# Keys and queries as one Strassen product, norms after the first keys, short node scans and mixed queries two chunks ahead in a graph-transformer layer

## Chip, cores, metric

One core of a Trainium2 chip. The metric is the device time of one execution in microseconds. Engines are named as the profile names them: PE (TensorE, matmul), PEld (its weight loads), DVE (VectorE), ACT (ScalarE), POOL (GpSimd), SP (SyncE, which here only issues transfers).

## What is computed

10,000 nodes with 512 features, 160,000 edges sorted by the node that they point to. All numbers are float32.

```python
xn = layernorm(x)
# node part: rows gathered at the edges' sources, weighted, summed per target
node = relu(segment_sum((xn @ W)[edge_src] * edge_weight[:, None], edge_dst) + bias)
# linear attention, 8 heads of 64
q, k, v = split(xn @ w_qkv.T, 3)
q = softmax(q, over the 64 features of a head) * 64 ** -0.5
k = softmax(k, over all nodes)
mix = gamma_layernorm(((k.T @ v) per head applied to q) @ w_out.T, gamma)
x = x + node + mix
# feed-forward with 6 experts of 341 units, weights of the experts from the mean row
x = x + ffn(layernorm(x))
```

The edges are sorted by `dst`, the target; `src` is random. The sum commutes with the product by `W`, so the kernel sums gathered rows of `xn` first and multiplies the sums (by `wg`) later.

## The kernel before

The nodes are worked on in 20 chunks of 512 rows (the last has 272); a chunk lies in a tile [128 partitions, 4 rows, 512]. P = 128, SUB = 4, KB = 4 blocks of 128 features, KH = 2. There are three stages.

**1. Normalised rows.** All chunks are read, normalised and stored to `xn_d` in HBM. The first EARLY = 3 stay in SBUF, in a pool of 3 buffers; the others go through 4 buffers.

```python
def normal_rows(n):
    for c in range(len(normal), min(len(normal) + n, NCH)):
        xt = (xp if c < EARLY else a_io).tile([P, SUB, D], F32, name="xn")
        nc.sync.dma_start(xt[:r], tokens(x, c))
        row_stats(xt, r, mv, on_pool=True)
        ...                                   # 2 of 4 rows on ScalarE, 2 on GpSimd
        nc.scalar.dma_start(tokens(xn_d, c), xt[:r])
```

**2. Keys, with the edges between.** Per chunk: keys and queries (16 matmuls of 128x512 each), exponentials, `G += ek.T @ xn` (16 more), and 32 transposes. `usable` is 1 where the weights' norms are small enough for exponentials without a maximum; it comes from two squares and 8 matmuls at the start.

```python
norms(0, wk); norms(1, wq); as_they_are()        # gives `usable`
for c, (_, r) in enumerate(chunks):
    if c == EARLY:
        normal_rows(NCH); place_edges(); ...
        done[1] = -6 * PACE                      # edges begin
    for s in range(SUB):
        times(pk, xnT, s, r, wk)                 # 4 matmuls 128x512
        work(KB * PRODUCT)                       # PRODUCT = 0.83
        nc.scalar.activation(ek[:r, s, :], pk[:r], AF.Exp, scale=usable[:r])
        nc.vector.tensor_tensor(kacc[:r], kacc[:r], ek[:r, s, :], ALU.add)
    for s in range(SUB):
        times(pq, xnT, s, r, wq)
        work(KB * PRODUCT)
        ...                                      # exp, softmax of each head -> qt
    xnT = turned_rows(c + 1, xn_next)            # 16 transposes
    for cb in range(KB):
        for s in range(SUB):
            nc.tensor.matmul(pc, ek[:r, s, cb * P : (cb + 1) * P], xn[:r, s, :], ...)
        ...                                      # G += pc, work(...), qt transposed and stored
    find_rows(c, added)
```

The order of instructions on PE is that of the program; the other engines' order comes from a scheduler. An edge tile is 128 edges. `work(us)` tells how much of PE's own work has been put out, and edge tiles are put out behind it, one per PACE = 0.93 of that sum:

```python
def edges_in(i):                                 # one gather per edge tile, 128 rows of 2 KB
    m[k] = pools["m"].tile([P, D], F32, name="msg")      # 24 buffers
    nc.gpsimd.indirect_dma_start(out=m[k], in_=xn_d, in_offset=...src_sb[:, t0 + k]...)
    nc.vector.tensor_scalar(sel[:, k, 1:], iota_w, place..., w_sb..., op0=is_equal, op1=mult)
def edges_summed(i, batch, m, sel):              # 4 windows of 32 nodes side by side on PE
    nc.tensor.matmul(pm[h * 32 : (h + 1) * 32, :], sel[:, k, :], m[k], ...)
    nc.scalar.copy(part, pm); nc.scalar.dma_start(part_d[...], part)
def work(us):
    done[1] += us
    edges_to(groups_of(int(done[1] / PACE)))
```

A node that lies on the edge between windows is put together by `carry`: two loads from `part_d`, a product, a store. `find_rows` finds for every node its row in `part_d`, by a scan of all 802 windows:

```python
for s in range(SUB):
    nc.vector.scalar_tensor_tensor(past, bases[:, :NW], node[:, c, s : s + 1], jump,
                                   op0=ALU.is_le, op1=ALU.mult, accum_out=at[:, s : s + 1])
```

**3. Nodes and queries, with the rest of the edges between.** `attention(c)` multiplies the stored queries with the mixing matrix; `gathered(c)` fetches the chunk's node rows, once `far_enough(c)` has put out the edges that they need (all of them from chunk 18 on, where the edge buffers are given up and the experts' weights are loaded).

```python
def attention(c, beside):
    qT = queries_in(c); xt = rows_again(c)
    for s in range(SUB):
        if s == SUB - 1:
            beside()
        times(po, qT, s, r, mix); put_out(KB * PRODUCT)
        ...                                      # layer norm, gamma, + x  -> ot

ot_next = attention(0, lambda: None)
for c, (_, r) in enumerate(chunks):
    ot, at = ot_next, held["at"]
    def nodes_rows():
        transposed(aT, at, r, psum, "ps", by_act=range(KB))
        if c + 1 < NCH:
            held["at"] = gathered(c + 1)         # 4 gathers of node rows
    if c + 1 < NCH:
        ot_next = attention(c + 1, nodes_rows)
    else:
        nodes_rows()
    for s in range(SUB):
        times(po, aT, s, r, wg); put_out(KB * PRODUCT)
        ...                                      # bias, relu, added to ot
    nc.sync.dma_start(x1_d[c], ot[:r])
```

**4. Feed-forward**, 20 chunks again, with Strassen's products already; the change leaves it as it is.

Of the kernel before, what the change touches and what calls it, by code (L numbers as in the profile page):

```python
# [17 lines left out]
P = 128  # L18
SQ = 32
SUB = 4  # L20
EPS = 1e-5
HEAD = 64
# [5 lines left out]
EARLY = 3  # L28
ROWS_SOON = 5
PRODUCT = 0.83  # L30
PACE = 0.93

# [14 lines left out]
def gps_layer_kernel(  # L47
# [55 lines left out]
    nc.gpsimd.memset(ones, 1.0)  # L103
    zero = const.tile([P, D], F32, name="zero")
    nc.vector.memset(zero, 0.0)
    iota_w = const.tile([P, WIN - 1], F32, name="iota_w")
# [42 lines left out]
    by_window = part_d.rearrange("(w q) d -> w q d", q=WIN)  # L149
    nc.scalar.dma_start(part_d[ZERO_ROW : ZERO_ROW + P, :], zero)  # L150

# [30 lines left out]

    def softmax_rows(q, r, s, e=None):

        q3 = q[:r, s, :].rearrange("p (h e) -> p h e", e=HEAD)
        e3 = q3 if e is None else e[:r].rearrange("p (h e) -> p h e", e=HEAD)
        qs = small.tile([P, D // HEAD], F32, name="qs")
        nc.vector.tensor_reduce(qs[:r], e3, axis=AX.X, op=ALU.add)
        nc.vector.reciprocal(qs[:r], qs[:r])
        nc.vector.tensor_tensor(q3, e3, qs[:r, :, None].to_broadcast([r, D // HEAD, HEAD]), ALU.mult)  # L190

# [35 lines left out]
    def sums_for(o, b11, b12, b21, b22):  # L227

        return [nc.vector.tensor_tensor(o[0], b12, b11, ALU.subtract),
                nc.vector.tensor_tensor(o[2], b22, b12, ALU.subtract),  # L230
                nc.vector.tensor_tensor(o[1], b22, o[0], ALU.subtract),
                nc.vector.tensor_tensor(o[3], b21, o[1], ALU.subtract)]

    io_f = {}
# [100 lines left out]
    with ExitStack() as ph:  # L335
# [10 lines left out]
        keys_ctx = ph.enter_context(ExitStack())  # L346
        xp = keys_ctx.enter_context(tc.tile_pool(name="b_xn", bufs=EARLY, side="right"))
        b_io = keys_ctx.enter_context(tc.tile_pool(name="b_io", bufs=1, side="right", reuse_waits="tile"))
# [8 lines left out]
        def normal_rows(n):  # L357

            for c in range(len(normal), min(len(normal) + n, NCH)):
                r = chunks[c][1]  # L360
                xt = (xp if c < EARLY else a_io).tile([P, SUB, D], F32, name="xn")
                nc.sync.dma_start(xt[:r], tokens(x, c))
                mv = small.tile([P, SUB, 2], F32, name="mv")
                row_stats(xt, r, mv, on_pool=True)
                minus = small.tile([P, SUB], F32, name="minus")
                nc.vector.tensor_scalar(minus[:r], mv[:r, :, 0], -1.0, None, op0=ALU.mult)
                for i in range(SUB):
                    if i % 2:
                        nc.gpsimd.tensor_scalar(xt[:r, i, :], xt[:r, i, :], mv[:r, i, 0:1], mv[:r, i, 1:2],
                                                op0=ALU.subtract, op1=ALU.mult)  # L370
                    else:
                        nc.scalar.activation(xt[:r, i, :], xt[:r, i, :], AF.Identity, bias=minus[:r, i : i + 1])
                        nc.scalar.activation(xt[:r, i, :], xt[:r, i, :], AF.Copy, scale=mv[:r, i, 1:2])
                nc.scalar.dma_start(tokens(xn_d, c), xt[:r])
                normal.append(xt)

        normal_rows(2)
        wk = kvp.tile([P, KB, D], F32, name="wk")
        nc.sync.dma_start(wk, w_qkv_t[:, D : 2 * D].rearrange("(k p) d -> p k d", p=P))
        nc.sync.dma_start(wq, w_qkv_t[:, :D].rearrange("(k p) d -> p k d", p=P))  # L380
        wv = kvp.tile([P, KB, D], F32, name="wv")
        wo = kvp.tile([P, KB, D], F32, name="wo")
        src_sb = ep.tile([P, NET], I32, name="src_sb")
# [4 lines left out]
        jump = ep.tile([P, NW], F32, name="jump")  # L388
        count = ep.tile([P, 2 + len(AT_HAND)], F32, name="count")
        n_big = ep.tile([1, 2], F32, name="n_big")  # L390
# [3 lines left out]
        def place_edges():  # L394
# [11 lines left out]
            nc.vector.tensor_copy(bases[:, PAIRED:NW], row_sb[:, 2 * PAIRED :])  # L406
            gap = ew.tile([P, NW], F32, name="gap", tag="past", bufs=1)
            nc.vector.tensor_tensor(gap, bases[:, 1:], bases[:, :NW], ALU.subtract)
# [29 lines left out]
            for i, (n, w) in enumerate(AT_HAND):  # L438
                nc.vector.tensor_scalar(count[:, 2 + i : 3 + i], bases[:, w : w + 1],
                                        float(chunks[n][0] if n < NCH else N), None, op0=ALU.is_ge)  # L440

        ALL_GOOD = P * (NET + NW - 1 + len(AT_HAND))

        def find_rows(c, other):

            at = ew.tile([P, SUB], F32, name="at")
            for s in range(SUB):
                past = ew.tile([P, NW], F32, name="past", bufs=1)
                scan = nc.vector.scalar_tensor_tensor(
                    past, bases[:, :NW], node[:, c, s : s + 1], jump,  # L450
                    op0=ALU.is_le, op1=ALU.mult, accum_out=at[:, s : s + 1])
                if other:
                    behind(scan, other)
            nc.vector.tensor_tensor(at, at, node[:, c], ALU.add)
            nc.vector.tensor_scalar(row_of[:, c], at, float(ZERO_ROW), None, op0=ALU.min)
# [60 lines left out]
        def norms(i, w):  # L516

            sq = b_io.tile([P, KB, D], F32, name="sq", tag="ek")
            nc.scalar.activation(sq, w, AF.Square)
            pn = psum.tile([1, D], F32, name="pn", tag="ps")  # L520
            for kb in range(KB):
# [3 lines left out]
        def as_they_are():  # L525
# [3 lines left out]
            nc.vector.tensor_tensor(n_big[:, 0:1], n_big[:, 0:1], n_big[:, 1:2], ALU.mult)  # L529
            pn = psum.tile([P, 1], F32, name="pn", tag="ps")  # L530
            nc.tensor.matmul(pn, until[0:1, :], n_big[:, 0:1], start=True, stop=True)
# [87 lines left out]
        def all_edges(fp):  # L619

            earlier = fp.tile([P, P], F32, name="earlier")
# [103 lines left out]
        def rows_of(c):  # L727
            if c < EARLY:
                return normal[c]
# [8 lines left out]

        norms(0, wk)
        norms(1, wq)  # L740
        as_they_are()
        xn = rows_of(0)
        xnT = turned_rows(0, xn)
        for c, (_, r) in enumerate(chunks):
            if c == EARLY:
# [4 lines left out]
                for soon in range(ROWS_SOON):  # L750
# [4 lines left out]
                                                                 reuse_waits="tile"))  # L755
                nc.sync.dma_start(wv, w_qkv_t[:, 2 * D :].rearrange("(k p) d -> p k d", p=P))
                nc.sync.dma_start(wo, w_out_t.rearrange("(k p) d -> p k d", p=P))
            if c + 1 < NCH:
                xn_next = rows_of(c + 1)
            ek = b_io.tile([P, SUB, D], F32, name="ek")  # L760
            for s in range(SUB):
                pk = psum.tile([P, D], F32, name="pk", tag="ps")
                times(pk, xnT, s, r, wk)
                work(KB * PRODUCT)
                nc.scalar.activation(ek[:r, s, :], pk[:r], AF.Exp, scale=usable[:r])
                nc.vector.tensor_tensor(kacc[:r], kacc[:r], ek[:r, s, :], ALU.add)
            qt = b_io.tile([P, SUB, D], F32, name="qt")
            for s in range(SUB):
                pq = psum.tile([P, D], F32, name="pq", tag="ps")
                times(pq, xnT, s, r, wq)  # L770
                work(KB * PRODUCT)
                nc.scalar.activation(pq[:r], pq[:r], AF.Exp, scale=usable[:r])
                softmax_rows(qt, r, s, pq)
            if c + 1 < NCH:
# [15 lines left out]
            if c >= ROWS_SOON:  # L790
                find_rows(c, added)
            if c + 1 < NCH:
                xn = xn_next
        ps = psum.tile([P, KB], F32, name="pks", tag="ps")
        for cb in range(KB):
# [81 lines left out]
        def rows_again(c):  # L877
            xt = io.tile([P, SUB, D], F32, name="xt")
            nc.sync.dma_start(xt[: chunks[c][1]], tokens(x, c))
# [8 lines left out]
        def attention(c, beside):  # L888
# [4 lines left out]
            xt = rows_again(c)  # L893
            ot = io.tile([P, SUB, D], F32, name="ot", bufs=3)
            for s in range(SUB):
# [16 lines left out]

        ot_next = attention(0, lambda: None)
        for c, (_, r) in enumerate(chunks):
            ot, at = ot_next, held["at"]
            aT = io.tile([P, KB, SUB * P], F32, name="aT", bufs=1)
# [5 lines left out]

            if c + 1 < NCH:
                ot_next = attention(c + 1, nodes_rows)
            else:
# [170 lines left out]
    hp = ctx.enter_context(tc.tile_pool(name="f_h", bufs=1, reuse_waits="tile"))  # L1096

    def product(o, lhs, rhs, start=True, stop=True):  # L1100
        n = len(lhs)
        for j in range(n):
            nc.tensor.matmul(o, lhs[j], rhs[j], start=start and j == 0, stop=stop and j == n - 1,  # L1103
                             skip_group_check=True)

# [215 lines left out]
```

## Time and profile before

| what | value |
|---|---|
| time, median of 3 runs | 3378.7 us (3378.27 to 3379.26) |
| span of the profile, mean granted TensorE clock | 3379.6 us, 0.988 |
| busy: PE, DVE, ACT, POOL | 97%, 55%, 24%, 42% |
| first product of chunk 0 and of chunk 3 (keys) | 43.0 us, 193.2 us |
| first and last gather of an edge tile | 169.9 us, 1903.3 us |
| end of the last chunk's keys, first query product | 1137 us, 1180.2 us |
| last node product of the last chunk ends | 2009.6 us |
| gathers of edge tiles, of node rows | 1250, 80 |

A busy share is an average over the four stages. In the page's slices (84 us each) the keys run to the fourteenth, with edges between them from the third on, nodes and queries to the twenty-fourth, feed-forward from there on. A line of a group reads: source line, engine, operation, output<-inputs, shapes, count, then busy us and mean ns of one, then the idle time of the engine before it and who ended it. In the timeline a line is start, length, engine, source line, operation, and in brackets the idle time before and its releaser. A PE matmul of float32 appears as two records. A gather's line on POOL tells how long POOL was at it, not when its data landed.

### The profile page before, as it was taken

How to read it: one execution, taken by the hardware profiler on the slowest of the kernel's cores; microseconds unless marked ns; L12 is line 12 of the kernel's file. 1: busy time of each engine (PE TensorE's matmuls, PEld its weight loads, DVE VectorE, ACT ScalarE, POOL GpSimd, SP SyncE). 2: the span in 40 equal slices, each digit the busy share in tenths (PEclk: the TensorE clock that was granted, in tenths of full speed). 3: DMA queues.
4: the chain of work that ended last, by engine and by line, in shares of the span. 5: the costliest groups of instructions: out<-in, count | busy, mean ns of one | idle time of the engine just before them, and what ended most of it. 6: DMA issues, size and time to landing. Idle time of an engine off the chain costs nothing.

```text
span 3379.6 us, 37367 instructions
## 1 busy us (share of the span) xinstructions
PE 3270.7 (97%) x12969; PEld 1923.8 (57%) x12969; DVE 1842.5 (55%) x4771; ACT 797.3 (24%) x1626; POOL 1433.4 (42%) x1472
## 2 busy tenths in 40 slices
PE   6999999999999899999999999999999999999998
PEld 3444444444443333333333347888888888888886
DVE  7844545455545456666766576544554455445543
ACT  4412121212121121122222123222222222222211
POOL 6667777777777777777777420000000000000000
PEclk9999999999999999999999999999999999999999
DMA  9778888888878888999989751121212121212111
GB/s 363 262 231 254 275 258 279 257 272 263 268 241 262 290 291 304 309 329 325 329 313 329 235 163 50 50 63 50 88 50 63 54 84 50 63 60 78 50 39 40
DMA packets 218332, 644.96 MB, mean 191 GB/s; under 512 B 35486, under 2 KB 75422, under 8 KB 193786
## 3 DMA queue, kind: packets, MB, share of 16 engines
q0 software_dynamic: 108208, 354.02, 33.5%
q1 hardware_dynamic: 67656, 168.51, 15.2%
q10 hardware_dynamic: 42266, 119.91, 9.1%
q8 instruction: 106, 1.74, 0.2%
q14 instruction: 96, 0.79, 0.1%
HBM read 485.32 MB, written 157.00 MB: 190 GB/s over the span
## 4 chain that ended last, share of the span: by engine, by line
PE 54%; DMA 9%; issue 1%; DVE 1%; POOL 1%; ACT 0%; POOLq 0%; DVEq 0%; ACTq 0%; SPq 0%
PE px L1103 15%; PE pz L1103 10%; PE py L1103 10%; PE po L205 7%; DMA msg<-xn_d,src_sb 6%; PE pg L205 6%; PE pm L503 3%; PE ph L1103 2%; PE pt L197 1%; DMA z_d<-xt 1%; POOL msg L485 1%; DMA xt<-x_d 1%; DMA at<-part_d,row_of 1%; DMA x_d<-ot 0%; PE pcarry L568 0%
## 5 line engine op out<-in xcount | busy, mean ns | idle before, releaser
L485 POOL DMA_INDIRECT msg<-xn_d,src_sb x1250 | 1226.5, 981 | 424.8 <-issue 236.6
L503 PE MATMUL pm<-msg,sel 128*32 128x512 f32 x2504 | 356.2, 603 | 28.7 <-DMA msg<-xn_d,src_sb 28.6
L492 DVE TENSOR_SCALAR sel<-iota_w,place,w_sb 128x31 f32<-128x31 f32 x1250 | 305.9, 317 | 103.9 <-PE pm L503 103.7
L205 PE MATMUL po<-G,qT 128*128 128x512 f32 (+1 forms) x640 | 292.7, 604 | 8.0 <-DMA qT<-qT_d 8.0
L205 PE MATMUL pg<-wq,aT 128*128 128x512 f32 (+1 forms) x640 | 293.5, 607 | 5.9 <-ACT aT L199 5.9
L779 PE MATMUL pc<-xn,ek 128*128 128x512 f32 (+1 forms) x640 | 288.7, 601 | 3.7 <-DVE qt L190 3.7
L205 PE MATMUL pk<-wk,xnT 128*128 128x512 f32 (+1 forms) x640 | 285.7, 599 | 0.0
L205 PE MATMUL pq<-wq,xnT 128*128 128x512 f32 (+1 forms) x640 | 284.5, 597 | 0.0
L506 ACT COPY part<-pm 128x512 f32<-128x512 f32 x201 | 118.1, 587 | 629.7 <-PE pm L503 604.7
L503 PEld LDWEIGHTS pm<-msg,sel 128*32 128x32 f32 x2504 | 68.3, 109 | 282.2 <-issue 196.9
L205 PEld LDWEIGHTS pg<-wq,aT 128*128 128x128 f32 (+1 forms) x640 | 116.9, 189 | 182.9 <-issue 162.9
L205 PEld LDWEIGHTS po<-G,qT 128*128 128x128 f32 (+1 forms) x640 | 116.0, 189 | 171.0 <-issue 147.5
L205 PEld LDWEIGHTS pk<-wk,xnT 128*128 128x128 f32 (+1 forms) x640 | 118.1, 188 | 164.4 <-issue 153.1
L205 PEld LDWEIGHTS pq<-wq,xnT 128*128 128x128 f32 (+1 forms) x640 | 117.5, 187 | 165.3 <-issue 159.2
L1103 PE MATMUL px<-xnT,w_sb 128*128 128x256 f32 (+1 forms) x800 | 203.8, 377 | 6.4 <-DVE u L1138 6.3
L779 PEld LDWEIGHTS pc<-xn,ek 128*128 128x128 f32 (+1 forms) x640 | 118.7, 192 | 145.8 <-issue 141.7
L1103 PE MATMUL px<-w_sb,hh 128*128 128x256 f32 (+1 forms) x800 | 185.7, 379 | 0.0
L161 DVE BATCH_NORM_STATS2 st<-ot 128x6 f32<-128x512 f32 (+1 forms) x160 | 110.2, 689 | 138.4 <-ACT ot L903 137.5
L1103 PE MATMUL py<-xs,w_sum 128*128 128x256 f32 (+1 forms) x800 | 185.0, 374 | 0.0
L1103 PE MATMUL py<-w_sum,hh 128*128 128x256 f32 (+1 forms) x800 | 179.2, 379 | 0.0
L1103 PEld LDWEIGHTS px<-xnT,w_sb 128*128 128x128 f32 x800 | 150.3, 191 | 28.5 <-DVE u L1138 8.8
L1103 PEld LDWEIGHTS py<-w_sum,hh 128*128 128x128 f32 (+1 forms) x800 | 150.0, 188 | 22.7
(270 smaller groups left out, 4438.5 us busy)
## 6 DMA issues: line engine op xcount, KB each, us to landing
part_d<-part ACTq DMA_DIRECT2D x201, 256.0 KB
msg<-xn_d,src_sb POOLq DMA_INDIRECT x1250
xn<-in_x SPq DMA_DIRECT2D x19, 1024.0 KB
xn_d<-xn ACTq DMA_DIRECT2D x19, 1024.0 KB
qT_d<-qT ACTq DMA_DIRECT2D x19, 1024.0 KB
qT<-qT_d SPq DMA_DIRECT2D x19, 1024.0 KB
xt<-in_x SPq DMA_DIRECT2D x19, 1024.0 KB
x_d<-ot SPq DMA_DIRECT2D x19, 1024.0 KB
```

What stands on the lines that cost most here:

```text
L161: nc.vector.bn_stats(st[:r, s, :], t[:r, s, :])
L197: nc.tensor.transpose(pt[:, s * r : (s + 1) * r], t[:r, s, kb * P : (kb + 1) * P], ident[:r, :r])
L205: nc.tensor.matmul(po[:r, :], t[:, kb, s * r : (s + 1) * r], w[:, kb, :], start=kb == 0, stop=kb == KB - 1)
L485: nc.gpsimd.indirect_dma_start(out=m[k], out_offset=None, in_=xn_d, in_offset=bass.IndirectOffsetOnAxis(ap=src_sb[:, t0 + k : t0 + k + 1], ...
L492: nc.vector.tensor_scalar(sel[:, k, 1:], iota_w, place[:, t0 + k : t0 + k + 1], w_sb[:, t0 + k : t0 + k + 1], op0=ALU.is_equal, op1=ALU.mult)
L503: nc.tensor.matmul(pm[h * WIN : (h + 1) * WIN, :], sel[:, k, :], m[k] if k < len(m) else m[0], start=j == 0, stop=j == batch - 1, skip_gro ...
L506: nc.scalar.copy(part, pm)
L779: nc.tensor.matmul(pc, ek[:r, s, cb * P : (cb + 1) * P], xn[:r, s, :], start=s == 0, stop=s == SUB - 1)
L1103: nc.tensor.matmul(o, lhs[j], rhs[j], start=start and j == 0, stop=stop and j == n - 1, skip_group_check=True)
```

## The change

1. **One Strassen product.** Rows of a chunk are taken in two halves, features in two halves, and keys and queries as the two column halves of one result. Seven products take the place of eight: 14 matmuls for a pair of rows where there were 16, for chunks 3 to 19. VectorE adds the parts up; the sums of the weights (`kq_sum`) are made once, those of the rows (`xs`) for each chunk. `wv` and `wo` share the buffer of `kq_sum`, so they are loaded after the keys.
2. **Norms behind the first keys.** The four key products of chunk 0 are put out before the norms; their exponentials wait for `usable`.
3. **Scans over few windows.** `find_rows` scans only the windows in which a chunk's nodes can lie (39 to 145 of 802, by the expected distribution with SPARE = 10 tiles on each side); two more comparisons per chunk check that.
4. **Mixed queries two chunks ahead.** `attention(c + 2)` stands where `attention(c + 1)` stood; `ot` has 4 buffers, `xt` 1.
5. Two kept chunks instead of three (KEPT), PACE 0.9 instead of 0.93.

```diff
-PACE = 0.93
+PACE = 0.9
+KEPT = 2
...
+    def seven(keys, queries, s, r, t, t_sum, w, w_sum, between):
+        h, s2 = 2 * r, s + SUB // 2
...
+        p6 = times_of(sa(1), sb(1))
+        product(first, a(0, 0), b(0, 0), stop=False)
+        nc.scalar.copy(u, first)
+        between(2)
+        add(u, u, p6)
+        p5 = times_of(sa(0), sb(0))
+        add(queries[:r, s, :], u, p5)
+        add(keys[:r, s2, :], u, times_of(sa(2), sb(2)))
+        between(2)
+        product(first, a(0, 1), b(1, 0), start=False)
+        add(queries[:r, s2, :], keys[:r, s2, :], p5)
+        add(queries[:r, s, :], queries[:r, s, :], times_of(sa(3), b(1, 1)))
+        add(keys[:r, s2, :], keys[:r, s2, :], times_of(a(1, 1), sb(3)))
+        between(3)
+        return first
...
-        xp = keys_ctx.enter_context(tc.tile_pool(name="b_xn", bufs=EARLY, side="right"))
+        xp = keys_ctx.enter_context(tc.tile_pool(name="b_xn", bufs=KEPT, side="right"))
...
+            lo, hi = span(c)
             for s in range(SUB):
-                past = ew.tile([P, NW], F32, name="past", bufs=1)
+                past = ew.tile([P, WIDEST], F32, name="past_c", bufs=1)[:, : hi - lo - 1]
                 scan = nc.vector.scalar_tensor_tensor(
-                    past, bases[:, :NW], node[:, c, s : s + 1], jump,
+                    past, bases[:, lo + 1 : hi], node[:, c, s : s + 1], jump[:, lo + 1 : hi],
                     op0=ALU.is_le, op1=ALU.mult, accum_out=at[:, s : s + 1])
...
-        norms(0, wk)
-        norms(1, wq)
-        as_they_are()
...
-                nc.sync.dma_start(wv, ...)       # and wo, at the start of chunk 3
...
+            if c < EARLY:
...                                              # as before, with the norms after chunk 0's keys
+            else:
+                xs = b_io.tile([P, 4, KH, HALF], F32, name="xs_b")
+                sums_of([xs[:, i, :, :h] for i in range(4)], xnT[:, :KH, :h], xnT[:, KH:, :h], ...)
+                for s in range(SUB // 2):
+                    first = seven(ek, qt, s, r, xnT, xs, (wk, wq), kq_sum, lambda n: work(n * KH * PRODUCT))
+                    s2 = s + SUB // 2
+                    nc.scalar.activation(ek[:r, s, :], first, AF.Exp, scale=usable[:r])
+                    nc.scalar.activation(ek[:r, s2, :], ek[:r, s2, :], AF.Exp, scale=usable[:r])
+                    ...                          # kacc, and the queries' exp and softmax
...
-            ot = io.tile([P, SUB, D], F32, name="ot", bufs=3)
+            ot = io.tile([P, SUB, D], F32, name="ot", bufs=4)
...
-        ot_next = attention(0, lambda: None)
+        mixed = [attention(c, lambda: None) for c in range(2)]
...
-            if c + 1 < NCH:
-                ot_next = attention(c + 1, nodes_rows)
+            if c + 2 < NCH:
+                mixed.append(attention(c + 2, nodes_rows))
```

## The prediction

> **What bounds the kernel now.** I read the page's slices first (PE busy in nine tenths nearly everywhere), then two stretches of equal length, then the list of groups, and last GpSimd's timeline. The two stretches, from the table of windows (busy us and instruction count of PE, weight loads, DVE, ACT, POOL, then clock, DMA share, GB/s):
>
> ```profile
> 600.00:700.00 100.00, 100.00 (x389) 42.56 (x391) 50.58 (x147) 19.15 (x31) 74.77 (x78) 1.00 0.85 269
> 1500.00:1600.00 100.00, 96.93 (x331) 35.23 (x330) 66.75 (x209) 23.07 (x45) 76.48 (x78) 1.00 0.95 329
> ```
>
> The first lies in the keys stage, the second in the node and query stage. PE counts as busy in both, but it starts 389 matmuls in one and 331 in the other: in the second it is waiting between them. POOL starts 78 instructions in both. Why 78, its timeline tells (start, length, idle before):
>
> ```profile
> 410.12 0.95 POOL L485 DMA_INDIRECT msg<-xn_d,src_sb  x1 [0.30 <-issue]
> 411.37 0.95 POOL L485 DMA_INDIRECT msg<-xn_d,src_sb  x1 [0.30 <-issue]
> 412.62 0.95 POOL L485 DMA_INDIRECT msg<-xn_d,src_sb  x1 [0.30 <-DMA msg<-xn_d,src_sb]
> 413.88 1.74 POOL L485 DMA_INDIRECT msg<-xn_d,src_sb  x1 [0.30 <-DMA msg<-xn_d,src_sb]
> 415.92 0.95 POOL L485 DMA_INDIRECT msg<-xn_d,src_sb  x1 [0.30 <-issue]
> ```
>
> 0.95 us for a gather and 0.30 us before the next, again and again: one gather per 1.254 us, at most 80 in 100 us. The 75% that the page shows as POOL's busy share is a full queue. 1250 gathers of edges and 72 of node rows run from 169.9 to 1904.3 us. 1322 times 1.254 is 1658 of these 1734 us. Adding up the timeline's exceptions gives the other 76: some 40 us of lengthened gathers, 28 us of waits for TensorE in the keys stage (13 of them in its first 60 us), 7 us of waits later. So **GpSimd's gather queue sets the length of everything between 170 and 1904 us**; in the keys stage PE is full as well. The feed-forward stage after 2010 us is PE's alone, and the change doesn't touch it.
>
> **What the Trainium skill says.** "Perfetto Trace Analysis", its opening note: matmul busy time is a bad metric as matmuls are pipelined; the trace agrees (331 against 389 starts at 97% and 100%). The same page, What "DMA-bound" means: a DMA whose issuing sequencer is solid with slices is bound by descriptor generation, not by moving data; the trace agrees, with 0.95 us gathers back to back and DMA engines at 0.85. "SBUF — State Buffer", Who interferes with whom: a VectorE instruction with two SBUF inputs contends with a GpSimd instruction that reads SBUF. The 1.74 us gathers at 413.9 and 417.2 lie beside the 1.05 us scans over `bases` and `jump`, which agrees; it doesn't show the mechanism. "TensorE: Matmul & The Clock Gate", Part 3: matmuls of 32 columns run side by side. The edge matmuls start 10 ns apart in fours, 16 records in some 1.72 us; I use that as 0.215 us of PE for an edge tile.
>
> **The change part by part.**
>
> *Strassen.* A 128x512 product is two records, 0.43 us from start to start. Chunks 3 to 19 now take 28 products for keys and queries in place of 32: 17 x 4 x 0.86 = 58 us of PE removed. It doesn't arrive whole. A chunk before: 96 records x 0.43 = 41.3, 32 transposes x 0.11 = 3.5, 42.6 edge tiles x 0.215 = 9.2, together 54.0; measured 55.9 (first products at 301.0 and 1083.6 us, 14 chunks), so 1.9 in switches. After: 88 x 0.43 = 37.8, 3.5, 40.6 tiles (44 products x 0.83 / 0.9) x 0.215 = 8.7, and 1.9: **51.9 us**. But 40.6 gathers need 40.6 x 1.28 (with the lengthened ones) = **52.0 us** of POOL. Both engines full, coupled by 24 message buffers: I take 53.0 us. VectorE gets 12 additions and 4 sums of 0.69 us in a chunk and loses most of 4.8 us of scans: from 28 to about 35 busy us of 53, which it can carry.
>
> *Start.* Before, the norms come ahead of everything on PE: the first transposes start at 39.6 and the first query products at 57.6 us. After, the keys can start when the first rows are normal (15.9 us, POOL): transposes to 20, keys to 34, then norms: 3.4 us of matmul, 2 for the square, 3.4, 5.6 for VectorE's answer, so queries at about 49. **-8 us**, chunk 3 at 185 instead of 193.2. The gathers start when the last normalised rows are stored (170). Two loads of 1 MB leave this time and the scans there shrink, but one buffer fewer holds rows; the last load stands behind the reload for chunk 3, which waits for chunk 1 and moves by those 8 us. So 162.
>
> *Keys to queries.* Keys end at 185 + 16 x 53 + 50.5 = 1084, not 1137. But the order of instructions on PE has 680 edge products by the end of the keys where it had 712, so with the buffers about 702 gathers are out, where 733 were. The 620 left, at the 1.302 us that one takes in the rest (767 us for 589), need 807 us: last gather at 1891, 13 us earlier than before. Of 53 us gained in the keys 40 are given back: **8 from the start and 5 more**.
>
> *Scans.* About 14 of the lengthened microseconds in the keys stage stand beside the scans. Two-input additions (`sums_of`, the softmax's product, now both from SBUF) replace some. **-3 us.**
>
> *Two chunks ahead.* On PE 88 products follow the last edge before, 60 after: 28 x 0.86 = 24 us less. The tail is a chain, though. Before, with L the last edge product (1917.3):
>
> ```profile
> 1917.31 8.15 PE L205 MATMUL pg<-wq,aT 128*128 128x512 f32 x16
> ...
> 1938.42 1.05 PE L574 MATMUL pcarry<-total,same 20*46 20x512 f32 x2
> ...
> 1940.22 0.23 ACTq L579 DMA_DIRECT2D part_d<-own  x1
> ...
> 1944.66 0.95 POOL L865 DMA_INDIRECT at<-part_d,row_of  x1 [40.30 <-DMA b_sb<-in_b]
> ...
> 1972.15 13.90 PE L205 MATMUL pg<-wq,aT 128*128 128x512 f32 x32
> ...
> 1993.78 15.98 PE L205 MATMUL pg<-wq,aT 128*68 128x512 f32 x32 [5.89 <-ACT aT L199]
> ```
>
> The carry stands 20 us behind L because products stand before it, and the gather of node rows waits for its store. After: 8 products and 16 transposes ahead of the carry, so it runs at L+14, store L+16, gather L+20; node product of chunk 17 to L+31, of 18 to about L+48, and the last one ends 23.7 us later as before (1985.9 to 2009.6): L+72 against L+92. **-20, say -21 us** with what the longer lead spares in single waits.
>
> Sum: -8 -5 -3 -21 = -37; 3378.7 - 37 = **3342 us**.
>
> **Rivals.** (a) PE was the only bound of the keys stage and its whole saving counts: 58 + 8 + 21, to 3292. For it: PE 100% busy there and 28 us of POOL's waits for PE. Against: 78 gathers in 100 us of a possible 80, in both stages. (b) VectorE becomes the bound: at a chunk's end it has accumulation, softmax, copies, the sums for the next chunk and selections, about 17 us of work beside 18 us of PE. Then a chunk stays near 55 us, POOL starves, 32 tiles are still left over, and the tail's gain alone shows: about 3372. For it: six PSUM banks that VectorE must empty. Against: half of its time is idle now. (c) Gathers run without any gap from 162 (1658 + 35): last one at 1855, end near 3307. Against: two engines so equally full lose time to each other. (d) DMA becomes the bound, 0.85 now and 0.95 later; the rate of gathers hardly rises (0.77 to 0.78 per us), so this matters least.
>
> **Range and chances.** (a) and (c) put the low edge, (b) the high one: 3314 to 3368. Over 2% means under 3311 us, which needs the gathers to be nearly gapless and the tail too: 0.1. Slower by over 2% would need the keys stage to be longer than before: 0.02. Same: 0.88.
>
> **What would show it.** Right: gathers still 1.25 us apart; first about 162, last about 1891; chunks of the keys 53 us apart; 331 or so PE starts in 100 us of the query stage; from last edge product to first feed-forward product 72 us; feed-forward unchanged at 1370 us. Wrong: gaps in POOL's queue in the keys stage with PE waiting for VectorE (b), or a last gather near 1855 (c), or a first gather not earlier than 170.

## The result, and the profile after

The changed kernel takes 3342.0 us (median of 4 runs, 3337.2 to 3348.2) against 3379.0 for the kernel before beside it (3378.3 to 3384.8): ratio 0.9888, 95% interval 0.9865 to 0.9911. A second set gave 3341.7 us, ratio 0.9889 (0.9873 to 0.9906). The gain, 1.1%, is clear of the noise and under the 2% that the prediction's chances take as a limit ("same"). The total is the one predicted. How it comes about is another matter: two terms of the sum were wrong by 10 us or more, with opposite signs, and the reason given for a third was only half of it.

The stretches of the changed kernel that answer to those shown of the kernel before (columns as there: busy us and count of PE, weight loads, DVE, ACT, POOL, then clock, DMA share, GB/s):

```profile
600.00:700.00 100.00, 100.00 (x394) 42.27 (x394) 67.08 (x190) 23.18 (x38) 76.24 (x79) 1.00 0.84 269
1500.00:1600.00 100.00, 95.08 (x333) 35.76 (x326) 61.88 (x188) 22.66 (x44) 76.11 (x78) 1.00 0.92 316
```

Still 79 and 78 gathers in 100 us, still 333 starts of PE in the query stage. Only DVE has more to do, in the keys stage (67 us where it was 51). GpSimd's timeline, in the same place as before:

```profile
410.18 0.95 POOL L556 DMA_INDIRECT msg<-xn_d,src_sb  x1 [0.30 <-issue]
411.43 0.95 POOL L556 DMA_INDIRECT msg<-xn_d,src_sb  x1 [0.30 <-issue]
412.68 0.94 POOL L556 DMA_INDIRECT msg<-xn_d,src_sb  x1 [0.30 <-PE pt L195]
413.93 1.40 POOL L556 DMA_INDIRECT msg<-xn_d,src_sb  x1 [0.31 <-PE pt L195]
```

The rate of the queue is the same. What changed is the exceptions: added up over the whole queue, GpSimd waits for TensorE 1.4 us (4.0 in the second profile, e12), where it was 31.7 in the kernel before (the idle time beyond the usual 0.30 us, where TensorE ended it). The longest two of these waits before:

```profile
208.40 1.02 POOL L485 DMA_INDIRECT msg<-xn_d,src_sb  x1 [8.03 <-PE pm L503]
...
1704.95 0.95 POOL L485 DMA_INDIRECT msg<-xn_d,src_sb  x1 [4.24 <-PE pcarry L574]
```

The first gather, however, comes no earlier (169.9 us before):

```profile
170.40 1.26 POOL L556 DMA_INDIRECT msg<-xn_d,src_sb  x1 [8.84 <-DMA xn_d<-xn]
```

It waits for the last store of normalised rows. The cause shows in SyncE's queue, where the last load of `x` stands alone, 10 us behind the reload of a chunk. Two lines of the kernel before, then two of the changed one:

```profile
99.85 38.08 SPq L362 DMA_DIRECT2D xn<-in_x  x6
141.30 0.35 SPq L731 DMA_DIRECT2D xn<-xn_d  x1
```

```profile
131.65 0.33 SPq L804 DMA_DIRECT2D xn<-xn_d  x1
141.88 0.34 SPq L412 DMA_DIRECT2D xn<-in_x  x1
```

PE's timeline at the end of the node stage, from the last edge product on (x32 are 16 products of 128x512):

```profile
1882.08 2.03 PE L574 MATMUL pm<-msg,sel 128*32 128x512 f32 x8 [0.47 <-DMA msg<-xn_d,src_sb]
1884.04 7.08 PE L203 MATMUL po<-G,qT 128*68 128x512 f32 x16
1890.96 1.91 PE L195 MATMUL pt<-ident,at 128*128 128x128 f32 x16
1894.63 1.02 PE L639 MATMUL pcarry<-on,same 46*46 46x512 f32 x2 [1.76 <-DMA on<-part_d]
1895.59 1.87 PE L645 MATMUL pcarry<-total,same 20*46 20x512 f32 x2
1897.39 6.18 PE L203 MATMUL po<-G,qT 128*68 128x512 f32 x8
1903.41 13.90 PE L203 MATMUL pg<-wq,aT 128*128 128x512 f32 x32
...
1918.89 13.90 PE L203 MATMUL pg<-wq,aT 128*128 128x512 f32 x32
...
1940.52 15.40 PE L203 MATMUL pg<-wq,aT 128*68 128x512 f32 x32 [1.06 <-ACT aT L197]
1955.76 1.03 PE L237 MATMUL px<-xs,w_sum 128*128 128x256 f32 x4
```

From the end of the last edge product, 1884.1 us, to the first feed-forward product: 71.6 us, where it was 92.2. Counting the records gives 60 products behind the last edge product, where there were 88.

Then something new, in the stage that the change doesn't touch. ScalarE's timeline, and PE's:

```profile
1966.99 0.37 ACT L1232 COPY u<-px 128x256 f32<-128x256 f32 x1 [8.17 <-DMA x_d<-ot]
```

```profile
1967.87 2.08 PE L237 MATMUL px<-xnT,w_sb 128*128 128x256 f32 x4 [6.77 <-DVE u L1233]
1969.74 3.53 PE L334 MATMUL pst<-stats,squares 128*128 128x80 f32 x16
```

The first copy out of a feed-forward product waits for the last store from `ot`; in the kernel before it did not:

```profile
2012.56 0.35 ACT L1137 COPY u<-px 128x256 f32<-128x256 f32 x1
```

PE, after 6.77 us of idleness, takes 2.08 us for what takes 1.03 elsewhere. From first feed-forward product to end: 1379.7 us, not 1370.0.

So in these two profiles (3379.6 and 3335.5 us): last edge product -33.3, tail -20.6, feed-forward +9.7.

### The profile page after: what moved, and what is told of

Read it like the earlier page. It is cut to its first block, busy times and chain, and to the rows that moved or that the text cites. A ratio compares the mean times of both kernels' runs of the same rounds, so it can differ in the third digit from the quotient of the medians.

```text
span 3335.5 us, 37444 instructions
## 1 busy us (share of the span) xinstructions
PE 3224.5 (97%) x12833; PEld 1903.5 (57%) x12833; DVE 1952.6 (59%) x5107; ACT 817.6 (25%) x1660; POOL 1427.1 (43%) x1472
## 4 chain that ended last, share of the span: by engine, by line
PE 58%; DMA 8%; DVE 2%; issue 0%; POOL 0%; ACT 0%; DVEq 0%; POOLq 0%; SPq 0%; ACTq 0%
PE px L237 15%; PE pz L237 10%; PE py L237 10%; PE po L203 8%; PE pg L203 7%; PE pm L574 4%; DMA msg<-xn_d,src_sb 4%; PE ph L237 2%; DMA z_d<-xt 1%; PE pt L195 1%; DMA xt<-x_d 1%; DMA qT<-qT_d 0%; DMA at<-part_d,row_of 0%; DVE xt L1295 0%; PE pcarry L639 0%
## 5 line engine op out<-in xcount | busy, mean ns | idle before, releaser
L574 PE MATMUL pm<-msg,sel 128*32 128x512 f32 x2504 | 365.1, 603 | 28.6 <-DMA msg<-xn_d,src_sb 27.4
L875 PEld LDWEIGHTS pc<-xn,ek 128*128 128x128 f32 (+1 forms) x640 | 117.1, 190 | 142.4 <-issue 133.0
L237 PE MATMUL p<-kq_sum,xs_b 128*128 128x512 f32 (+1 forms) x408 | 189.5, 600 | 0.0
L237 PEld LDWEIGHTS px<-w_sb,hh 128*128 128x128 f32 (+1 forms) x800 | 150.0, 188 | 22.7
L237 PEld LDWEIGHTS py<-xs,w_sum 128*128 128x128 f32 x800 | 150.1, 191 | 20.0
L348 ACT ACTIVATE xn<-xn,st_all 128x128 f32<-128x128 f32 x288 | 114.8, 481 | 103.0 <-DMA xn<-x_d 103.0
```

The source lines that it names most:

```text
L348: nc.scalar.activation(xn[:, s, b * P : (b + 1) * P], xn[:, s, b * P : (b + 1) * P], AF.Identity, bias=st[:, b, s, 0:1], scale=st[:, b, s, ...
L574: nc.tensor.matmul(pm[h * WIN : (h + 1) * WIN, :], sel[:, k, :], m[k] if k < len(m) else m[0], start=j == 0, stop=j == batch - 1, skip_gro ...
```

## Experiments

One table for all, read from each profile: the last gather of edges, the end of the last edge product (L), the products of PE between L and the first feed-forward product, the length of that tail, the feed-forward stage, all in us but the count; then the median time. The comparison with the kernel before, on the same chip, stands with the experiments as a ratio (e7 0.9800, 0.9772 to 0.9829; e8 0.9639, 0.9608 to 0.9669).

| kernel | last gather | L | products left | tail | feed-forward | time |
|---|---|---|---|---|---|---|
| before | 1903.3 | 1917.4 | 88 | 92.2 | 1370.0 | 3379.0 |
| after | 1872.3 | 1884.1 | 60 | 71.6 | 1379.7 | 3342.0 |
| e1 after, plain products | 1861.0 | 1873.3 | 132 | 133.7 | 1379.9 | 3390.0 |
| e2 before, PACE 0.9 | 1884.9 | 1898.3 | 132 | 133.0 | 1368.1 | 3400.4 |
| e3 before, two ahead | 1900.6 | 1912.7 | 88 | 93.4 | 1376.9 | 3389.0 |
| e4 after, scratch moved | 1879.0 | 1894.3 | 60 | 69.1 | 1368.9 | 3335.5 |
| e5 Strassen, PACE 0.93 | 1903.2 | 1921.1 | 68 | 87.2 | 1370.2 | 3380.5 |
| e6 as e4, PACE 0.93 | 1887.5 | 1904.9 | 52 | 73.7 | 1369.5 | 3353.7 |
| e7 before, half the gathers | 1779.8 | 1845.5 | 88 | 91.6 | 1371.4 | 3310.9 |
| e8 after, half the gathers | 1733.2 | 1800.0 | 60 | 70.5 | 1380.8 | 3256.3 |
| e9 after, one ahead | 1872.9 | 1896.5 | 68 | 83.8 | 1368.4 | 3348.9 |
| e10 Strassen, PACE 0.9 | 1868.5 | 1892.1 | 68 | 83.8 | 1367.4 | 3347.1 |
| e11 as e4, again | 1877.6 | 1888.4 | 60 | 72.3 | 1369.4 | 3335.3 |
| e12 after, again | 1873.9 | 1890.5 | 60 | 69.3 | 1379.8 | 3341.7 |

Theory 1, that of the prediction: GpSimd's queue sets the length of everything up to the last gather. Rival 1 below: TensorE's work does, and Strassen's 58 us come back as they are when it is taken out.

**e1: Strassen taken back.**

```diff
-            if c < EARLY:
+            if c < NCH:                          # plain products for all chunks
```

> The changed kernel, but chunks 3 to 19 take the plain products again (32 of 128x512 for keys and queries of a chunk, not 28); everything else, PACE 0.9 too, stays. Theory 1, GpSimd's queue of gathers sets the length from 170 to 1872 us and TensorE's saving is not what shortens it: a chunk of the keys takes some 57 us (44.3 edge tiles by 1.28 us) and not 51.8, so the keys end some 80 us later than 1054, but some 60 more gathers are out by then; the last gather stays within 10 us of 1872 us and the time within 10 us of the changed kernel's 3342. Rival 1, TensorE bounds the keys stage: the 58 us of products come back whole, near 3400 us.

3390.0 us (3387.9 to 3395.0), ratio to before 1.0025 (1.0011 to 1.0039). The queue did as theory 1 says: it has no gaps, 751 gathers are out by the end of the keys, the last comes at 1861, even earlier than in the changed kernel. Yet the time is 48 us longer. The tail is why: 132 products behind the last edge product, 133.7 us. The queue alone doesn't set the time; the rival's 3400 is nearer than theory 1's 3342.

**e2: PACE alone**, on the kernel before.

```diff
-PACE = 0.93
+PACE = 0.9
```

> The kernel before with PACE 0.9 in place of 0.93 and nothing else. Theory 1: edge tiles are put out 3% sooner against TensorE's products, so GpSimd never runs dry in the keys stage; the 15 us that it waited for TensorE after the first 60 us of that stage go, and the time falls by 10 to 15 us, to about 3366. Rival 1 (TensorE bounds that stage): no change, 3379, or a little longer as more edge products stand among the keys. Rival 2: this number, not Strassen, brings the whole part of the gain that comes before the last gather, 30 us: 3349.

3400.4 us, ratio 1.0055 (1.0038 to 1.0072): 21 us slower, which none of the three expected. Again the part about the queue held: GpSimd's waits for TensorE in the keys, behind their first 60 us, went from 15 us to 2, and the last gather came 18 us earlier. PE's timeline tells what that is worth:

```profile
1184.77 4.14 PE L503 MATMUL pm<-msg,sel 128*32 128x512 f32 x10 [0.82 <-DMA msg<-xn_d,src_sb]
...
1897.19 1.07 PE L503 MATMUL pm<-msg,sel 128*32 128x512 f32 x8
...
1903.42 13.90 PE L205 MATMUL pg<-wq,aT 128*128 128x512 f32 x32
...
1932.64 13.90 PE L205 MATMUL pg<-wq,aT 128*128 128x512 f32 x32
...
1964.02 13.90 PE L205 MATMUL pg<-wq,aT 128*128 128x512 f32 x32
...
1993.23 13.90 PE L205 MATMUL pg<-wq,aT 128*128 128x512 f32 x32
...
2014.86 16.59 PE L205 MATMUL pg<-wq,aT 128*68 128x512 f32 x32 [5.89 <-ACT aT L199]
```

Five chunks' node products stand behind the last edge product; before it was three and a half (112 records of `pg`). Edge tiles called earlier made PE wait for their gathers (PE's order is fixed). The first line shows it: 10 records take 4.14 us where 8 take 1.07 at 1897. From the end of the keys to the first query product it is 54.9 us, where it was 44.1, and in the query stage the record of an edge product takes 0.178 us from start to start, where it was 0.160. And the products that could have covered these waits were left for the end, when GpSimd had nothing more to do: L 19 us earlier, tail 41 us longer.

**e3: two chunks ahead alone**, on the kernel before.

```diff
-            if c + 1 < NCH:
-                ot_next = attention(c + 1, nodes_rows)
+            if c + 2 < NCH:
+                mixed.append(attention(c + 2, nodes_rows))   # ot: 4 buffers, xt: 1
```

> The kernel before with the mixed queries two chunks ahead (4 buffers of ot, 1 of xt) and nothing else. Theory 1: the last gather stays at 1903 us; from the last edge product to the first feed-forward product 72 us in place of 92; then, since the layout of ot is that of the changed kernel, the first feed-forward chunk may lose the 9 us that it lost there (a copy on ScalarE that waits for the last store of the node stage). Sum: 20 us less without that loss (3359), 11 with it (3368).

3389.0 us, ratio 1.0032 (1.0022 to 1.0043). The tail is 93.4 us, as it was, and so are the 88 products in it. The tail of the kernel before is no chain: PE is idle in it for 5.9 us only. And the feed-forward lost 6.9 us in its profile, which leaves some 4 of the 11 us by which the time grew unexplained. The -20 us of the prediction are not to be had by this part alone.

**e4: the scratch elsewhere.**

```diff
+    sp = ctx.enter_context(tc.tile_pool(name="f_s", ...))   # u and the like: now ahead
     fp = ctx.enter_context(tc.tile_pool(name="f_io", ...))
     w2_sum = fp.tile(...)
-    sp = ctx.enter_context(tc.tile_pool(name="f_s", ...))
```

> The changed kernel with one pool of the feed-forward stage (the scratch that the copies of products go to) placed ahead of two others, so that it doesn't lie where the last ot buffer lay. If the 9.7 us by which the feed-forward stage grew are that copy's 8.17 us wait for the store from ot, with TensorE's clock halved behind it, the wait goes, the first feed-forward chunk takes 85 us in place of 95, and the time falls by 7 to 10 us from 3342. If the growth has another cause (a longer stretch of full power before, later weights), it stays within 2 us of the changed kernel.

3335.5 us, ratio 0.9873 (0.9857 to 0.9889); feed-forward 1368.9 us. The cause of its growth is settled: with the fourth buffer of `ot`, `u` came to lie on rows still being stored. The wait, 8.1 to 8.2 us, stands in all five profiles with four buffers and the scratch in its old place (after, e1, e3, e8, e12), and in none of the other nine.

After these four runs I turned to theory 2: TensorE's own work in its fixed order sets the time everywhere, and gathers count only where PE waits for a message.

**e5: Strassen alone** (with short scans and two kept chunks).

```diff
-PACE = 0.9
+PACE = 0.93
+        norms(0, wk); norms(1, wq); as_they_are()    # ahead of the keys again; ot: 3 buffers, xt: 2
-                mixed.append(attention(c + 2, nodes_rows))
+                ot_next = attention(c + 1, nodes_rows)
```

> The changed kernel with three of its parts taken back: PACE 0.93, norms ahead of the keys, mixed queries one chunk ahead. What is left of the change is Strassen's product (with its two kept chunks) and the short scans. Theory 2, formed after the first four runs: TensorE's own work in its fixed order sets the time in all stages, and the gathers count only where TensorE waits for a message; then the 58 us of products arrive nearly whole, less what TensorE waits more in the query stage as the keys end 56 us earlier: 3321 to 3335. Theory 1 (the queue of gathers sets the length): the queue starts at 170 us as before and keeps its waits, 3365 to 3379.

3380.5 us, ratio 1.0008 (0.9997 to 1.0019): 58 us of PE's work less, and nothing to show for it. Theory 2 fell as theory 1 had, though theory 1's number for this run, 3365 to 3379, is close. The keys did end at 1053.5 us, 83 us earlier than before; but edge tiles are put out by products, fewer products call fewer tiles, and GpSimd still starves in the keys. Its timeline:

```profile
299.21 0.94 POOL L556 DMA_INDIRECT msg<-xn_d,src_sb  x1 [4.37 <-PE pm L574]
...
601.82 0.94 POOL L556 DMA_INDIRECT msg<-xn_d,src_sb  x1 [2.63 <-PE pm L574]
...
623.09 0.94 POOL L556 DMA_INDIRECT msg<-xn_d,src_sb  x1 [1.47 <-PE pm L574]
```

GpSimd's waits for TensorE sum to 20.8 us in the keys and 9.4 later, about what they were before (26.3 and 5.5). 672 gathers are out by the end of the keys (732 before), and the last one comes at 1903.2 us, to a tenth where it was. PE's 58 us became waiting: an edge product's record takes 0.187 us in the query stage, where it was 0.160, and PE's idle time is longer too (42 us before edge products, where it was 27; 17 in the tail, where it was 6). The table of windows:

```profile
600.00:700.00 100.00, 100.00 (x395) 42.46 (x394) 66.38 (x190) 23.25 (x37) 74.13 (x76) 1.00 0.81 260
1500.00:1600.00 100.00, 94.17 (x305) 33.23 (x304) 62.10 (x192) 20.54 (x39) 75.14 (x76) 0.98 0.92 313
```

305 starts of PE in the query stage, where there were 331.

**e6: the changed kernel with PACE 0.93** (and the scratch of e4).

> The changed kernel with the scratch pool placed first (3335 us) and PACE 0.93 in place of 0.9. Theory 2: PACE 0.9 alone cost the kernel before 21 us, because edge products called early wait for gathers and leave products of their own for the end; here 0.93 should give back some 10 us: 3322 to 3330, with less idle time of TensorE before edge products in the query stage and a later last gather. Theory 1: GpSimd runs dry in the keys stage again and the time grows by some 10 us, 3345.

3353.7 us, ratio 0.9929 (0.9906 to 0.9952): 18 us more than e4. Theory 2 had the sign wrong (3322 to 3330); theory 1 had too little (3345), but named what is found: GpSimd waits for TensorE in the keys again, 15.0 us (e4: none), and the last gather comes 8.5 us later. The same PACE that costs the plain kernel 21 us is worth 18 here.

**e7 and e8: half the gathers.** An odd tile's product takes the rows of the even one before it. All products stay; what is left out is 625 of 1250 gathers, and with them the rows that the output needs.

```diff
-                    if k < n:
+                    if k < n and k % 2:
+                        m[k] = m[k - 1]
+                    elif k < n:
                         m[k] = ...                   # the gather
```

> The kernel before with every second gather of an edge tile left out (its product takes the rows of the tile before it), so that 625 gathers of edges run in place of 1250; all products stay. Theory 2: TensorE's waits for messages go, 27 us of idle time before edge products and some 40 us by which these take longer in the query stage than in the keys stage, and little else: 3310 to 3335. Theory 1: the 0.9 ms of POOL time saved free the whole stretch until another engine binds, well over 100 us less.

> The changed kernel with the same gathers left out. Theory 2: its waits go too (25 us idle, 45 us in longer edge products), 3270 to 3290; the distance to the kernel before with half its gathers stays that of TensorE's work, 58 us of products and some 10 to 15 at the start, less the 10 us lost to the scratch copy: 40 to 60. Theory 1: half the gathers uncover the saving that the queue hid, and the distance grows from 37 to 85.

3310.9 us (3310.3 to 3311.5) and 3256.3 us (3253.0 to 3259.6). Rows of the list of groups, e7 and then e8:

```profile
L487 POOL DMA_INDIRECT msg<-xn_d,src_sb x625 | 611.7, 979 | 904.9 <-PE pm L505 722.8
```

```profile
L558 POOL DMA_INDIRECT msg<-xn_d,src_sb x625 | 623.2, 997 | 844.6 <-PE pm L576 680.7
```

GpSimd now sits idle for most of the time, and TensorE waits for no gather: no idle time is left before edge products in the query stage. That gives the cost of the queue, with the transfers that it starts (half of these go too, and the runs don't separate the two): 3379.0 - 3310.9 = 68 us in the kernel before, 3342.0 - 3256.3 = 86 us in the changed one (84 by the ratios). e7 is at the low end of what theory 2 expected. e8 fell further than I expected (3270 at the lowest), so the changed kernel hangs more on its queue than the kernel before does. The distance between the two, 55 us, and 64 if the 9.4 us of the scratch are added, fits what the change takes from TensorE's work, Strassen's 58 and some at the start, and not the 85 of theory 1.

Theory 3, from these eight: TensorE's own work is within 2 to 3% of the whole time (68 of 3379, 86 of 3342), with GpSimd's queue just ahead of it. **The node stage ends at the end of the gather queue plus what PE has left behind the last edge product**, and PACE decides how much of that there is. Too early: a long remainder (132 products). Too late: the queue starves. Strassen takes 68 products out, and only a kernel that has them out can put edges earlier without piling up a remainder.

**e9: the changed kernel, one chunk ahead; e10: Strassen and PACE 0.9 without the two other parts** (e5 with PACE 0.9).

> The changed kernel with the mixed queries one chunk ahead, as before the change (3 buffers of ot, 2 of xt); Strassen's product, PACE 0.9 and the norms behind the first keys stay. Theory 3, formed after eight runs: the node stage ends at the end of the gather queue plus what TensorE still has behind the last edge product, which is its products left over by PACE or, if they are few, the carry chain. On TensorE 68 products follow the last edge product here, as in the kernel with Strassen alone, whose tail was 87 us; the gathers run without gaps as in the changed kernel, to some 1875 us; no buffer of ot lies under the scratch, so the feed-forward takes 1370 us. Sum: first feed-forward product near 1973, time 3336 to 3346, the same as with two ahead. Rival: two chunks ahead is worth the 20 us that the prediction gave it, 3360.

> As the kernel before, but with Strassen's product, the short scans and PACE 0.9: norms ahead of the keys, mixed queries one chunk ahead. It closes the table of Strassen with and without, PACE 0.93 and 0.9. Theory 3: no waits of GpSimd for TensorE (18.7 and 7.5 us in the kernel with PACE 0.93), last gather near 1880 us, 68 products behind the last edge product as there, tail 87: 3345 to 3355, while each of the two alone brought nothing. If the two parts simply add, +1 and +21 us: 3400.

e10: 3347.1 us, ratio 0.9912 (0.9895 to 0.9929). The table is closed:

| | PACE 0.93 | PACE 0.9 |
|---|---|---|
| plain products | 3379 | 3400 |
| Strassen | 3380 | 3347 |

Each alone brings nothing or a loss, both together 31 us. They can't be added; theory 3 had 3345 to 3355, from waits that were to vanish: GpSimd's fell from 30.2 us to 9.4. (The lower row has the short scans and two kept chunks as well; these weren't taken apart.)

e9: 3348.9 us, ratio 0.9915 (0.9898 to 0.9932), over the 3336 to 3346 expected. It differs from e10 by the place of the norms alone and is no faster: the norms behind the first keys bring nothing. PE starts on chunk 0 at 12.6 us and not at 36.9, but the gathers start at 173.1 and not at 168.6. From e9 to the changed kernel is the step of two chunks ahead: first feed-forward product 20 to 24 us earlier (1980.3 against 1955.8 and 1959.8), feed-forward 11 us longer, 7 us net. Theory 3 had expected no difference. So up to the feed-forward that part has the size predicted for it, but only beside Strassen and PACE 0.9, where few products are left; in e3 the 88 products stayed, and so did the tail. Of the 20 to 24 us, 12 to 14 lie in the tail; the others lie ahead of it, where theory 3 has no term: in e9 L stands 23.6 us behind the last gather, in the changed kernel 11.8. PE has no idle time there in e9; its order puts products of its own between the last edge tiles.

**e11 and e12: the moved scratch and the changed kernel side by side.**

> The changed kernel with the scratch pool placed first, once more and beside the changed kernel itself on one chip: 3332 to 3340, 6 to 10 us under the changed kernel, if the wait for the last store is all that it takes away.

> The changed kernel unaltered, on the same chip as the one with the moved scratch: 3340 to 3348, with the 8 us wait before the first copy of the feed-forward stage.

3335.3 us (3331.9 to 3340.4) against 3341.7 (3337.7 to 3342.1); ratios to before 0.9878 (0.9862 to 0.9895) and 0.9889 (0.9873 to 0.9906). The difference of the means is 5.1 +- 5.1 us, and both sets (e4, e11 against the two of the changed kernel) say 6. ScalarE's timeline of e11:

```profile
1963.76 0.35 ACT L1232 COPY u<-px 128x256 f32<-128x256 f32 x1
```

No wait any more. This version is the fastest of those with all gathers, by a difference to the changed kernel that in this pair alone just reaches the edge of the noise.

## Why the prediction was right, and where it wasn't

- **First gather 162 (-8): wrong.** 170.4 and 171.8 us. The text noted that the last load of `x` stands behind a reload and let both move by 8 us; in fact that last load left at 141.9, later than any load before, and undid the gain. The keys did start earlier (chunk 3 on PE near 178 us against 193). e9 beside e10 confirms that the norms' place is worth nothing. The fewer kept rows alone don't hold that load back: e5 and e10 keep two chunks as well but have the norms ahead, and there no load is left behind the reload (e10: the six loads are out by 134.3, the reload follows at 138.4). It takes the earlier keys: all eight profiles with the norms behind the first keys have the late load. Whether these do it with three kept chunks too was not run.
- **A chunk of the keys 53 us: 51.8.** The bound by TensorE was worked out as 51.9, and that is what came; the extra microsecond for "both engines full, coupled by 24 message buffers" wasn't there. (The four edge matmuls of a group start 6 to 7 ns apart, not 10; the 0.215 us for a tile doesn't depend on it.)
- **"40 are given back", last gather 1891: the term that was mis-sized.** It came at 1872 to 1874. The number of gathers out by the end of the keys (702 predicted, 691 found) and the pace afterwards (1.302 us predicted; (1872.3 - 1054.2) / 631 = 1.297) were nearly right. But the keys ended at 1054, not 1084: 7 us from the start of chunk 3, the rest from the 16 chunks behind it, 1.4 us each in the mean. 691 gathers by then mean a queue almost without a gap: the 28 us of waits for TensorE, for which the working allowed, fell to 1.4. That is near rival (c), a gapless queue, from a start at 170. e2, e5 and e10 show what removes most of them: PACE 0.9 (31.7 to 15.0 us in the plain kernel, 30.2 to 9.4 beside Strassen), at a cost in time in the plain kernel and with a gain beside Strassen. With the norms behind the first keys as well (e9) 2.9 are left.
- **Scans -3: right in the keys stage, gone in the sum.** Before, 49 gathers ran beside scans and took 1.24 us in the mean; after, 27 ran beside the short ones, took 0.95 us, and none was lengthened. Gathers beside the new additions of two tiles in SBUF (into `xs`) took 1.05 to 1.13 us. In the keys the lengthening (what gathers over 1.0 us take beyond 0.95) fell from 21.5 to 16.1 us, but over all gathers of edges it is 40.4 before and 40.5 after (37.4 in e12, the same kernel).
- **Two ahead -20 to -21, tail 72: the number right, the reason half.** 71.6 and 69.3 us. "88 products follow the last edge before, 60 after" was put down to the order alone, and the tail was called a chain. e3 shows that the order alone keeps 88; e5 and e10 that Strassen brings 68, and e9 that two ahead brings the last 8 and the shorter chain (PE is idle in the tail for 13.8 us in e9, 6.3 in the changed kernel). With 5.9 us of idle time before and 6.3 after, products fill the tail of both kernels. 68 (one ahead) and 52 (two ahead, as in e6) are the least that can stand there: all edges must be out before chunk 18's rows are fetched, and what follows that point is fixed.
- **Feed-forward unchanged at 1370: wrong, 1379.7.** e4 and e11 show the cause and take it away. The fourth buffer of `ot` was in the diff; I didn't ask what would lie there later.
- **Rival (a)**, all of Strassen's saving counts, failed: 3292 against 3342. But "78 gathers in 100 us of a possible 80" was no argument that TensorE doesn't matter: without Strassen (e1) the time is 48 us longer. **Rivals (b) and (d)**: a chunk's 51.8 us leave no room for a VectorE bound, and gathers run at their old rate with DMA at 0.92 in the query stage; whether the transfers hold back TensorE there was not tested apart from the queue.

Taken together, in the first profile: L came 33 us earlier where 16 were expected, the tail as expected, feed-forward 10 us later where none was expected: 44 us, in the fastest of the four executions. In the second profile (e12) it is 27, 23 and 10: 40 us. The prediction's 37 agrees with the medians by luck: two errors of opposite sign, 11 to 17 us and 10, nearly cancel.

## What to carry to other kernels

Where two engines are both within a few per cent of the bound, don't credit a saving on one of them by itself: ask what the other needs in order to follow, and look at what each still has to do when the other is finished. A knob that sets the rate of one against the other (PACE here) has to be set again after every change of work; of the two values tried, the better one for the old kernel was the worse for the new. And when a buffer is added, look at what is placed on that memory in the next stage.

## What the runs showed of the hardware that I hadn't expected

**A wait is paid for again in the clock.** After PE's 6.77 us of idleness in the changed kernel (1.05 at this place before) the granted clock stays low well beyond the wait. So of the 9.7 us by which the stage grew, 5.7 are idle time and some 4 are left for the slower clock (an estimate, the difference of these figures). The table of windows:

```profile
1956.00:1964.00 8.00, 5.10 (x24) 4.16 (x22) 5.17 (x15) 0.20 (x1) 0.00 (x0) 1.00 0.49 156
1964.00:1977.00 13.00, 9.13 (x30) 7.96 (x31) 3.89 (x8) 4.29 (x9) 0.00 (x0) 0.50 0.30 110
1977.00:1990.00 13.00, 13.00 (x51) 8.21 (x50) 5.41 (x12) 8.48 (x22) 0.00 (x0) 0.98 0.00 1
```

The Trainium skill, "TensorE: Matmul & The Clock Gate", Part 1, says that the clock falls to a half after an idle window of some 3.4 us and rises after some 3.4 us of sustained work. The half is what this trace shows (0.50). The rise came later than that here: products start again at 1967.9, four records that begin at 1974.9 still take 1.9 us, and the clock rises at 1977.6, after 9.7 us of work. In all five profiles with this wait it is 9.2 to 9.9 us.

**A full query stage hides its waits in PE's busy time.** From start to start, idle time left out, an edge product's record costs 0.116 us of PE in the keys and 0.160 in the query stage of the kernel before (the pace at which they start); with half the gathers it is 0.122 there. Over the query stage's 984 records the difference between 0.160 and 0.122 is 37 us that no list of waits shows. The warning about busy time of matmuls in the opening note of "Perfetto Trace Analysis" (the Trainium skill), which the prediction cites, applies to waits as well. Counting starts is a rough measure of them: of the 58 by which the prediction's two stretches differ, 23 are short transposes.
